# A four-layer graph network kernel: keys and queries of the top-p attention made while the features are made, second step on features already multiplied by U

## The chip, the cores and the metric

The kernel runs on one core of a Trainium2 chip. The metric is the device time of one launch in microseconds (us); lower is better. All data is float32, apart from a few throw-away outputs in bfloat16.

The engines that matter here: TensorE (PE in the profile, its weight loads PEld), VectorE (DVE), ScalarE (ACT), GpSimd (POOL) and SyncE (SP), which here only issues DMAs. Each engine runs its own list of instructions strictly in order and waits on semaphores for the results of others. PE's clock is granted by a throttle: 1.00 is full speed, 0.50 half.

## The reference, cut to what matters

A graph of n = 3327 nodes has features x (n x 256) and a sparse weight matrix adj (n x n, about 1% of its entries not zero, stored in full). Four layers follow each other, each with a residual and a layer normalization: x = layernorm(x + layer(x)). Layer 0 aggregates neighbours, layer 1 is a graph convolution with a Mamba scan, layer 2 a graph attention, layer 3 is this:

```
R = S + eye(N);  R = R / R.sum(-1, keepdims=True)        # S is adj
Z = 0; Xf = X; Xa = X
for n in range(2):
    q = Xa @ W1.T @ W2.T;  k = Xa @ W3.T                 # N x 64 each
    A = softmax(q @ k.T), in each row only the largest entries up to
        a mass of 0.9 are kept, then each row is divided by its sum
    Xf = R @ Xf
    Xa = A @ Xa
    Z = Z + Xf @ U1[n].T + Xa @ U2[n].T
return layernorm(X + Z)
```

The change concerns layers 2 and 3 alone. Layer 3 has two kinds of large products per step: the diffusion R @ Xf, and the attention A @ Xa, whose matrix A must first be made: logits, softmax, and for every row the threshold that keeps 0.9 of the mass (the search).

## The kernel before, in words

Nodes are cut into nt = 26 row tiles of 128. X, the features, stays in SBUF as 26 tiles of 128 x 256; adj is streamed, transposed by the host, tile by tile, in every stage that needs it: a row tile needs 26 blocks of 128 x 128. The code is written in order of tiles; a scheduler then gives each engine a fixed order of its instructions, and it does move work of neighbouring tiles past each other. Tiles of memory come from pools with a fixed number of buffers, which sets how far a load or a copy may run ahead.

**Layer 2** (`layer2`, L516 on): for each row tile, two halves of 13 blocks are loaded, DVE makes the weights from each in place (two operations on 128 x 1664), and 26 matmuls add up `acc` (L549). Then, per tile, a chain over DVE, ACT and POOL makes the new X: L552 to L561 on DVE and ACT, mean and variance at L77 and L78, the power on POOL (L565, L566), and last `X` on POOL (L567). Adding `acc` takes 26 matmuls, each of them two records in the trace.

**Layer 3** is two calls of `one_pass` (L927): pass 1 with X as attention source, `search_short` and `first`; pass 2 with Xa, `search_long` and `second`. A pass goes:

- `keys` (L607): for all 26 tiles, one after another, two transposes (L94), a copy on ACT (L96), two matmuls with W3 (L613), a copy into kT (L615). Nothing else of the pass can start before it. The weights W1, U1, U2, W2, W3 are loaded ahead of pass 1 (L61, L581, L582), after layer 2 in SP's queue.
- per tile `query` (L618): transposes, W1 (L622), W2 (L626), with an ACT copy after each; `logits` (L631): eight matmuls (L642), 416 columns wide, contraction of 64, each copied by ACT into `e` (L643).
- the search. `search_short` (L685): the eight largest of each segment of 128 (L650), six rounds of ranking (L659, L661), one exponential over the row (L668) that also gives the sum, then the threshold v and the masked row. `search_long` (L697) is in three stages, which run for three different tiles in each step of the loop (lead 2, 1, 0): stage 1 makes two exponentials (L712, L713); stage 2 estimates a threshold with a Sign count and a masked sum (L723, L725), then a better one with Relu and Sign (L747, L748); stage 3, from L750 on, takes the count, masks (L769), ranks, settles ties (L788) and masks again (L789).
- the attention product, `attend` (L111): the row tile `e` is transposed in 26 pieces (L118), copied out in groups of four (L120) and multiplied with X or Xa (L122). L805 scales the sum.
- the diffusion, `diffuse` (L864) with `aggregate` (L99): loads of 9 blocks, 26 matmuls (L107), and L869 adds the tile itself.
- in pass 2, `finish` (L877): four sources are transposed (L94, L96) and multiplied by U1 and U2 of both steps, eight matmuls (L884); then two layer normalizations (L886 to L897), and the store.
- at the pass's end `unresolved` (L901) finds whether a certificate of the search fails for any tile. The flag is read by all engines (L946), and a branch would run such tiles again in an exact and slow way.

Of the kernel before, what the change touches and what calls it, by code (L numbers as in the profile page):

```python
# [15 lines left out]
PSUM = bass.MemoryType.PSUM  # L16

# [14 lines left out]
LN15 = math.log(1.5)  # L32
# [3 lines left out]
HUGE = 1e38  # L36
KC = 416
# [3 lines left out]
def gnn_kernel(ctx: ExitStack, tc: tile.TileContext, n: int, a: dict, out: bass.AP):  # L41
# [369 lines left out]
    def layer2_any():  # L411

        with tc.tile_pool(name="l2", bufs=1) as pool, tc.tile_pool(name="l2w", bufs=2) as work, \
                tc.tile_pool(name="l2p", bufs=3, space=PSUM) as psum:
            wg = load(pool, "gat_w")
            asr, ads = (load_row(pool, x) for x in ("attn_src", "attn_dst"))
            H = pool.tile([P, nt, D], F32, name="H")
            col = pool.tile([P, nt, 2], F32, name="col")
            src = pool.tile([P, npad], F32, name="src")
            mv_all = pool.tile([P, nt, 2], F32, name="mv_all")  # L420
            rs_all = pool.tile([P, nt], F32, name="rs_all")
            for it in range(nt):
                xt = transposed(work, psum, X[:, it, :], "xt")
                po = psum.tile([P, D], F32, name="acc")
                for k in range(2):
                    nc.tensor.matmul(po, xt[:, k, :], wg[:, k, :], start=(k == 0), stop=(k == 1))
                nc.scalar.copy(H[:, it, :], po)
                for k, v in enumerate((asr, ads)):
                    scr = work.tile([P, D], F32, name="scr")
                    nc.vector.scalar_tensor_tensor(scr, H[:, it, :], 1.0, v, op0=ALU.mult, op1=ALU.mult,  # L430
                                                   accum_out=col[:, it, k:k + 1])

            for j0 in range(0, nt, 4):
                m = min(4, nt - j0)
                pt = psum.tile([P, 4, P], F32, name="ps")
                for j in range(m):
                    nc.tensor.transpose(pt[:, j, :], col[:, j0 + j, 0:1].to_broadcast([P, P]), ident)
                nc.scalar.copy(src[:, j0 * P:(j0 + m) * P], pt[:, :m, :].rearrange("p a b -> p (a b)"))
            for it in range(nt):
                ad = work.tile([P, n], F32, name="ad")  # L440
                nc.sync.dma_start(ad, a["adj"][it * P:(it + 1) * P, :])
                s = work.tile([P, npad], F32, name="s", bufs=3)
                if npad > n:
                    nc.vector.memset(s[:, n:], 0.0)
                sn = s[:, :n]
                nc.scalar.activation(sn, src[:, :n], AF.Identity, bias=col[:, it, 1:2])
                nc.vector.scalar_tensor_tensor(sn, sn, 0.2, sn, op0=ALU.mult, op1=ALU.max)
                nc.vector.scalar_tensor_tensor(sn, ad, 0.0, sn, op0=ALU.is_gt, op1=ALU.mult)
                neg = small.tile([P, 1], F32, name="neg")
                nc.vector.reduce_max(neg, sn, axis=AX.X)  # L450
                nc.vector.tensor_scalar_mul(neg, neg, -1.0)
                nc.scalar.activation(sn, sn, AF.Exp, bias=neg)
                den = small.tile([P, 1], F32, name="den")
                nc.vector.scalar_tensor_tensor(sn, ad, 0.0, sn, op0=ALU.is_gt, op1=ALU.mult, accum_out=den)
                nc.vector.tensor_scalar_add(den, den, 1e-8)
                nc.vector.reciprocal(den, den)
                acc = attend(work, psum, s, H)
                o = work.tile([P, D], F32, name="o")
                nc.vector.tensor_scalar_mul(o, acc, den)

                ex = work.tile([P, D], F32, name="ex")
                nc.vector.tensor_scalar_min(ex, o, 0.0)
                nc.scalar.activation(ex, ex, AF.Exp)
                nc.vector.scalar_tensor_tensor(o, o, 0.0, X[:, it, :], op0=ALU.max, op1=ALU.add)
                nc.vector.scalar_tensor_tensor(X[:, it, :], ex, -1.0, o, op0=ALU.add, op1=ALU.add)
                stats(mv_all[:, it, :], X[:, it, :])
            rstd_of(rs_all, mv_all[:, :, 1])
            for it in range(nt):
                standardize(X[:, it, :], X[:, it, :], mv_all[:, it, 0:1], rs_all[:, it:it + 1])
# [6 lines left out]
    with tc.tile_pool(name="l2c", bufs=1) as pool:  # L476
        col = pool.tile([P, nt, 2], F32, name="col")
        V = pool.tile([P, nt, D + 1], F32, name="V")
        fit = pool.tile([1, 1], I32, name="fit")
        with tc.tile_pool(name="l2a", bufs=1) as wpool, tc.tile_pool(name="l2w", bufs=2) as work, \  # L480
                tc.tile_pool(name="l2p", bufs=3, space=PSUM) as psum:
            wg = wpool.tile([P, 2, D + 2], F32, name="wg")
            nc.sync.dma_start(wg[:, :, :D], a["gat_w"])
            for k, v in enumerate(("attn_src", "attn_dst")):
                r = load_row(wpool, v)
                for i in range(2):
                    scr = work.tile([P, D], F32, name="scr")
                    nc.vector.scalar_tensor_tensor(scr, wg[:, i, :D], 1.0, r, op0=ALU.mult, op1=ALU.mult,
                                                   accum_out=wg[:, i, D + k:D + k + 1])
            for it in range(nt):  # L490
                xt = transposed(work, psum, X[:, it, :], "xt")
                po = psum.tile([P, D + 2], F32, name="acc")
                for k in range(2):
                    nc.tensor.matmul(po, xt[:, k, :], wg[:, k, :], start=(k == 0), stop=(k == 1))
                nc.vector.tensor_copy(col[:, it, :], po[:, D:])
                g = V[:, it, D:]
                nc.scalar.activation(g, col[:, it, 0:1], AF.Exp, scale=0.2)
                nc.scalar.mul(V[:, it, :D], po[:, :D], g)

            big = wpool.tile([P, nt, 2], F32, name="big")  # L500
            nc.scalar.activation(big, col, AF.Abs)
            m = wpool.tile([P, 2], F32, name="m")
            nc.vector.reduce_max(m, big.rearrange("p t k -> p k t"), axis=AX.X)
            pm = psum.tile([2, P], F32, name="ps")
            nc.tensor.transpose(pm, m, ident)
            m2 = wpool.tile([2, 1], F32, name="m2")
            nc.vector.reduce_max(m2, pm, axis=AX.X)
            one = wpool.tile([2, 1], F32, name="one")
            nc.vector.memset(one, 1.0)
            ps = psum.tile([1, 1], F32, name="ps")  # L510
            nc.tensor.matmul(ps, m2, one, start=True, stop=True)
            f = wpool.tile([1, 1], F32, name="f")
            nc.vector.tensor_scalar(f, ps, BIG, None, op0=ALU.is_le)
            nc.vector.tensor_copy(fit, f)

        def layer2():  # L516
            with tc.tile_pool(name="l2", bufs=1) as pool, tc.tile_pool(name="l2w", bufs=2) as work, \
                    tc.tile_pool(name="l2at", bufs=5) as atp, \
                    tc.tile_pool(name="l2p", bufs=3, space=PSUM) as psum:
                q = pool.tile([P, nt], F32, name="q")  # L520
                nc.scalar.activation(q, col[:, :, 0], AF.Exp, scale=0.8)
                eps = pool.tile([P, nt], F32, name="eps")
                nc.scalar.activation(eps, col[:, :, 1], AF.Exp, scale=-1.0)
                nc.vector.tensor_scalar_mul(eps, eps, 1e-8)
                mhalf = pool.tile([P, 1], F32, name="mhalf")
                nc.vector.memset(mhalf, -0.5)

                r = pool.tile([P, npad], F32, name="r")
                for j0 in range(0, nt, 4):
                    m = min(4, nt - j0)  # L530
                    pt = psum.tile([P, 4, P], F32, name="ps")
                    for j in range(m):
                        nc.tensor.transpose(pt[:, j, :], col[:, j0 + j, 1:2].to_broadcast([P, P]), ident)
                    nc.scalar.activation(r[:, j0 * P:(j0 + m) * P], pt[:, :m, :].rearrange("p a b -> p (a b)"),
                                         AF.Exp, scale=-0.8)
                for it in range(nt):
# [493 lines left out]
```

## Time and profile before

| | |
|---|---|
| median of 3 runs | 4331.85 us (4331.15 to 4336.95) |
| the profiled execution | 4330.06 us |
| its span, first to last instruction | 4327.9 us |
| mean granted PE clock | 0.927 |
| PE busy | 3880.5 us, 90% |
| DVE busy | 2795.9 us, 65% |
| ACT busy | 1731.7 us, 40% |
| POOL busy | 276.6 us, 6% |
| moved by DMA | 239.33 MB, mean 55 GB/s |

The stages, in us from the span's start: layer 0 to 361; layer 1 and the projection of layer 2 to about 1830; layer 2's aggregation 1855.8 to 2149.9; keys of pass 1 to 2223.2; pass 1 to 3095.2; flag and keys of pass 2 to 3163.2; pass 2 to 4327.9.

How to read the profile: busy times are sums over the whole span, and an engine can be busy in one stage and wait in the next, so the stages are read apart. A row of a group gives line, engine, operation, output and inputs, how often, then busy time and mean, then the idle time that this engine had just before such instructions and what ended it. In a line of the timeline the first number is the start, the second the time from that start to the end of the group, and the bracket is the idle time before it and its releaser.

### The profile page before, as it was taken

The numbers are of one execution on the slowest core, as the hardware profiler recorded it, in microseconds if no ns is written. First come the engines' busy times: TensorE is split into PE (matmuls) and PEld (weight loads), VectorE is DVE, ScalarE is ACT, GpSimd is POOL, SyncE is SP. The second block draws the span as 40 slices with busy tenths as digits, with TensorE's granted clock in tenths as the row PEclk, the third lists the DMA queues.
The fourth block names the chain that finished last, engine by engine and source line by source line (L and its number), as shares of the span: only waits on it lengthen the run. The fifth ranks groups of instructions, "written<-read, shape, count | busy, mean of one in ns | idle before, by whom it ended". The sixth has DMA issues, their size and how long they took to land. (4 is left out here: it accounts for less than half of the span.)

```text
span 4327.9 us, 42860 instructions
## 1 busy us (share of the span) xinstructions
PE 3880.5 (90%) x15597; PEld 2791.7 (65%) x15597; DVE 2795.9 (65%) x6159; ACT 1731.7 (40%) x2826; POOL 276.6 (6%) x344
## 2 busy tenths in 40 slices
PE   8998999999999977799889999999868889888988
PEld 7886644444444433588767777777646767676767
DVE  1111588888888899688624444444158877787784
ACT  0001444444444544510033333333265656565652
POOL 0000000000000010133300000000000000000000
PEclk9998898989898988899969999999869999999999
DMA  5443211111111000044301111111101111111111
GB/s 180 136 141 98 68 37 32 37 32 32 32 32 32 21 0 0 21 159 152 131 16 48 48 53 59 48 48 49 32 0 51 41 46 40 46 40 46 41 45 37
DMA packets 67053, 239.33 MB, mean 55 GB/s; under 512 B 8434, under 2 KB 22770, under 8 KB 66690
## 3 DMA queue, kind: packets, MB, share of 16 engines
q1 hardware_dynamic: 66818, 236.37, 17.1%
q8 instruction: 127, 2.08, 0.2%
q14 instruction: 108, 0.88, 0.1%
HBM read 232.93 MB, written 3.41 MB: 55 GB/s over the span
## 5 line engine op out<-in xcount | busy, mean ns | idle before, releaser
L393 PE MATMUL y<-h,ident 128*128 128x512 f32 (+1 forms) x896 | 466.4, 671 | 91.3 <-DVE h L342 91.3
L339 DVE TENSOR_TENSOR_SCAN h<-dA,carry,db 128x512 f32<-128x512 f32 (+1 forms) x448 | 511.6, 1193 | 4.8 <-DVE db L336 0.5
L328 ACT ACTIVATE dA<-dt,A_log 128x512 f32<-128x512 f32 (+1 forms) x448 | 281.4, 684 | 350.8 <-DVE h L339 333.1
L393 PEld LDWEIGHTS y<-h,ident 128*128 128x128 f32 x896 | 192.2, 225 | 354.2 <-issue 206.4
L204 PE MATMUL cb<-X,at 128*128 128x256 f32 x1352 | 334.6, 403 | 26.9 <-ACT h L221 14.7
L204 PEld LDWEIGHTS cb<-X,at 128*128 128x128 f32 x1352 | 270.1, 203 | 113.7 <-issue 52.2
L122 PE MATMUL acc<-Xa,wt 128*128 128x256 f32 x1352 | 322.3, 391 | 19.3 <-ACT wt L120 18.9
L122 PE MATMUL acc<-X,wt 128*128 128x256 f32 x1352 | 310.1, 383 | 10.7 <-ACT wt L120 8.7
L107 PE MATMUL acc<-xa,at 128*128 128x257 f32 x1352 | 308.3, 381 | 0.0
L107 PE MATMUL acc<-Xf,at 128*128 128x256 f32 x1352 | 307.6, 379 | 0.0
L107 PE MATMUL acc<-X,at 128*128 128x256 f32 x1352 | 304.3, 379 | 0.0
L122 PEld LDWEIGHTS acc<-Xa,wt 128*128 128x128 f32 x1352 | 260.4, 196 | 67.3 <-ACT wt L120 31.9
L642 PE MATMUL ps<-kT,q 64*128 64x416 f32 x832 | 254.8, 595 | 54.2 <-ACT e L643 31.6
L549 PE MATMUL acc<-V,at 128*128 128x257 f32 x1352 | 294.2, 379 | 1.4 <-DVE at L546 1.4
L336 DVE TENSOR_TENSOR db<-du,row 128x2048 f32<-128x2048 f32 (+1 forms) x112 | 238.9, 2133 | 82.8 <-ACT row L324 82.6
L122 PEld LDWEIGHTS acc<-X,wt 128*128 128x128 f32 x1352 | 252.4, 190 | 59.5 <-ACT wt L120 27.3
L549 PEld LDWEIGHTS acc<-V,at 128*128 128x128 f32 x1352 | 255.8, 189 | 39.8 <-DVE at L546 1.8
L107 PEld LDWEIGHTS acc<-xa,at 128*128 128x128 f32 x1352 | 255.6, 191 | 37.5 <-issue 0.7
L96 ACT COPY xt<-ps 128x256 f32<-128x256 f32 x234 | 82.0, 373 | 491.3 <-PE ps L94 436.8
L107 PEld LDWEIGHTS acc<-X,at 128*128 128x128 f32 x1352 | 253.0, 190 | 32.3
L107 PEld LDWEIGHTS acc<-Xf,at 128*128 128x128 f32 x1352 | 251.4, 190 | 31.3
L321 PE MATMUL ps<-dbc,ident 48*128 48x512 f32 (+1 forms) x448 | 234.3, 637 | 20.3 <-ACT row L324 19.8
(273 smaller groups left out, 5698.6 us busy)
## 6 DMA issues: line engine op xcount, KB each, us to landing
at<-in_adjT SPq DMA_DIRECT2D x156, 576.0 KB, 3.7
at<-in_adjT SPq DMA_DIRECT2D x104, 832.0 KB, 4.4
at<-in_adjT SPq DMA_DIRECT2D x78, 512.0 KB, 3.5
xa<-in_x SPq DMA_DIRECT2D x1, 3328.0 KB, 12.7
xt<-in_xT SPq DMA_DIRECT2D x26, 128.0 KB, 3.9
out<-h SPq DMA_DIRECT2D x25, 128.0 KB, 1.7
w_in<-in_w_in SPq DMA_DIRECT2D x1, 1024.0 KB, 5.4
U<-in_U SPq DMA_DIRECT2D x2, 512.0 KB, 6.1
```

Of the source, the lines that this page charges most:

```text
L96: nc.scalar.copy(t, pt)
L107: nc.tensor.matmul(acc, at[:, j, :], rhs[:, j0 + j, :], start=(j0 + j == 0), stop=(j0 + j == nt - 1))
L122: nc.tensor.matmul(acc, wt[:, j, :], rhs[:, j0 + j, :], start=(j0 + j == 0), stop=(j0 + j == nt - 1))
L204: nc.tensor.matmul(acc, at[:, j % JC, :], X0[:, j, :], start=(j == 0), stop=(j == nt - 1))
L321: nc.tensor.matmul(ps[:, :w], ident[:R, r:r + 1].to_broadcast([R, P]), dbc[:, :w], start=True, stop=True)
L328: nc.scalar.activation(dA[:, g, :], dt[:, g, :], AF.Exp, scale=A[:, g, s:s + 1])
L336: nc.vector.tensor_mul(db, du, bc[0])
L339: nc.vector.tensor_tensor_scan(h[:, g, :], dA[:, g, :], db[:, g, :], initial=carry[:, s, g:g + 1], op0=ALU.mult, op1=ALU.add)
L393: nc.tensor.matmul(ys[g][:, :w], ident, h[:, g, :], start=(s == 0), stop=(s == DS - 1))
L549: nc.tensor.matmul(acc, at[:, j, :], V[:, j0 + j, :], start=(j0 + j == 0), stop=(j0 + j == nt - 1))
L642: nc.tensor.matmul(pl[:, :w], q[a:a + DA, :], kT[a:a + DA, c0:c0 + w], start=True, stop=True)
```

## The change

Nothing is approximated: the same sums are made in another order. The new code

- makes `wq`, the product of W1 and W2, once before layer 2, and loads W1, W2 and W3 there (ahead of layer 2's weights in SP's queue);
- in layer 2, after the first 13 matmuls of tile `it`, makes key and query of tile `it - 1` for pass 1 (`project`). The key goes to `kT[0]`, the query to DRAM (`qd`), from which each pass loads one tile at a time;
- in pass 1, makes in `first`, for every tile and directly from Xf and Xa of this tile: s = X + Xf U1[0] + Xa U2[0], which goes to DRAM (`sd`); Y = Xf U1[1]; G = Xa U2[1]; and key and query of the tile for pass 2;
- in pass 2, diffuses Y and applies the attention to G, so that their sum with s is already X + Z: `second` has no matmuls and no transposes, and only the layer normalizations;
- runs the diffusion up to DL = 4 tiles ahead and in groups of J3 = 7 blocks, one group after each pair of logits matmuls (`both`); `first` and `second` of a tile end one step of the loop later;
- has no barrier between the passes; the flags of both are tested once, at the end (L1051 of the new file);
- in `search_long`, puts some scalar steps that don't need the second count ahead of the end of stage 2; the exponential of pass 1 has no offset any more.

The exact path for flagged tiles and the other path of layer 2 (`layer2_any`) are changed to suit. The diff, cut to its core:

```diff
+        wk = pool.tile([P, 2, 2 * DA], F32, name="wk")
+        wq = pool.tile([P, 2, 2 * DA], F32, name="wq")
...
+        def key_and_query(work, ps, p, it, xt):
+
+            for k in range(2):
+                nc.tensor.matmul(ps[:, 0, :], wk[:, k, :], xt[:, k, :], start=(k == 0), stop=(k == 1))
+            h, j = divmod(it * P, half)
+            nc.scalar.copy(kT[p][h * DA:(h + 1) * DA, j:j + P], ps[h * DA:(h + 1) * DA, 0, :])
+            nc.sync.dma_start(qd[p][it], query(work, ps[:, 1, :], xt))
...
+                    def project(it):
+                        xt = transposed(work, psum, X[:, it, :], "xt")
+                        key_and_query(work, psum.tile([P, 2, P], F32, name="ps"), 0, it, xt)
...
+                            if j0 == 0 and it:
+                                project(it - 1)
...
+                    project(nt - 1)
...
-        def keys(work, psum, xs):
...
-        def query(work, psum, xs, it):
...
-        def finish(work, psum, it, xf2, xa2):
...
+        def aggregated(atp, psum, it, rhs):
+
+            acc = psum.tile([P, D], F32, name="acc")
+            for j0 in range(0, nt, J3):
...
+                yield None
+            yield acc
...
+        def diffused(work, atp, psum, p, it, out):
+
+            rd = rdeg[:, it:it + 1]
+            t = work.tile([P, D], F32, name="t")
+            nc.gpsimd.tensor_scalar(t, (Y if p else X)[:, it, :], rd, None, op0=ALU.mult)
+            if p:
+                s = work.tile([P, D], F32, name="s")
+                nc.sync.dma_start(s, sd[it])
+                nc.gpsimd.tensor_tensor(t, t, s, op=ALU.add)
+            for acc in aggregated(atp, psum, it, Y if p else X):
+                if acc is None:
+                    yield
+            d = work.tile([P, D], F32, name="xf", bufs=DL + 2)
+            nc.vector.scalar_tensor_tensor(d, acc, rd, t, op0=ALU.mult, op1=ALU.add)
+            out.append(d)
...
+        def first(work, psum, it, acc, f, xf):
+
+            xa = work.tile([P, D], F32, name="xa")
+            nc.scalar.mul(xa, acc, f)
+            yield
+            pt = psum.tile([P, 4, P], F32, name="pj")
+            for i, v in enumerate((xf, xa)):
+                for k in range(2):
+                    nc.tensor.transpose(pt[:, 2 * i + k, :], v[:, k * P:(k + 1) * P], ident)
+            xt = work.tile([P, 4, P], F32, name="xt", bufs=1)
+            nc.scalar.copy(xt, pt)
...
+            for k in range(4):
+                nc.tensor.matmul(ps[:, 0, :], xt[:, k, :], (u1 if k < 2 else u2)[:, 0, k % 2, :],
+                                 start=(k == 0), stop=(k == 3))
+            for k in range(2):
+                nc.tensor.matmul(ps[:, 1, :], xt[:, k, :], u1[:, 1, k, :], start=(k == 0), stop=(k == 1))
+            for k in range(2):
+                nc.tensor.matmul(pg[:, 0, :], xt[:, 2 + k, :], u2[:, 1, k, :], start=(k == 0), stop=(k == 1))
+            s = work.tile([P, D], F32, name="s")
+            nc.vector.tensor_add(s, ps[:, 0, :], X[:, it, :])
+            nc.sync.dma_start(sd[it], s)
+            nc.scalar.copy(Y[:, it, :], ps[:, 1, :])
+            nc.scalar.copy(G[:, it, :], pg[:, 0, :])
+            key_and_query(work, pg[:, 1, :].rearrange("p (a b) -> p a b", a=2), 1, it, xt[:, 2:, :])
+            yield
+
+        def second(work, psum, it, acc, f, xf):
+
+            h = work.tile([P, D], F32, name="h")
+            nc.vector.scalar_tensor_tensor(h, acc, f, xf, op0=ALU.mult, op1=ALU.add)
+            yield
...
+            for p, search, step, lead in ((0, search_short, first, (1,)), (1, search_long, second, (2, 1, 0))):
+                es, searches, xfs, todo = {}, {}, [], None
+                for i in range(-lead[0], nt):
+                    t = i + lead[0]
+                    parts = []
+                    if t < nt:
+                        q = work.tile([2 * DA, P], F32, name="q")
+                        nc.sync.dma_start(q, qd[p][t])
+                        es[t] = work.tile([P, npad], F32, name="e", bufs=3)
...
+                        parts.append(scores(work, psum, p, q, es[t]))
+                    more = range(len(xfs), min(nt, i + DL + 1))
+                    for j in more[:1]:
+                        parts.append(diffused(work, atp, psum, p, j, xfs))
+                    both(*parts)
+                    for part in lead:
+                        if 0 <= i + part < nt:
+                            next(searches[i + part])
+                    for j in more[1:]:
+                        both(diffused(work, atp, psum, p, j, xfs))
+                    if todo is not None:
+                        next(todo)
+                    if i >= 0:
...
+                        todo = step(work, psum, i, attended(work, psum, es[i], G if p else X), f, xfs[i])
+                        next(todo)
+                next(todo)
...
-        one_pass(X, search_short, first, (1,))
-        one_pass(Xa, search_long, second, (2, 1, 0))
```

## The prediction, made before the change had run

> **What bounds the kernel now.** The span is 4327.9 us; the profiled execution took 4330.06 us, so 2.2 us lie around the span, and it stands 1.8 us under the median of 4331.85. I first cut the span into stages (windows: length; then busy us of PE, PEld, DVE, ACT, POOL; then PE's clock, DMA share and GB/s).
>
> ```profile
> 1830.00:2150.00 320.00, 314.96 (x1453) 272.97 (x1452) 246.10 (x299) 35.33 (x99) 96.56 (x75) 0.99 0.41 139
> 2150.00:2223.00 73.00, 45.17 (x164) 33.88 (x164) 3.44 (x42) 19.22 (x58) 3.93 (x8) 0.53 0.14 45
> 2223.00:3098.00 875.00, 829.45 (x3998) 662.54 (x3998) 394.99 (x1414) 306.06 (x570) 24.39 (x47) 1.00 0.16 49
> 3098.00:3165.00 67.00, 47.26 (x169) 35.05 (x170) 0.00 (x0) 17.33 (x56) 1.77 (x5) 0.52 0.00 1
> 3165.00:4328.00 1163.00, 1004.60 (x4618) 789.68 (x4617) 885.56 (x3000) 659.36 (x881) 86.40 (x177) 0.94 0.13 40
> ```
>
> Layer 2's aggregation (row 1) and pass 1 (row 3) are PE at full clock with little slack: 11.4 and 33.4 us per tile of 26. Rows 2 and 4 make keys, serially, at half clock. Pass 2 (row 5) is busy on PE for 86%, DVE 76%, ACT 57%: none is full, engines wait for each other. Next I read the starts of the two serial stages and one DVE wait of pass 2 on the timeline, and the list of waits for that pass (us in total, times, longest).
>
> ```profile
> 2164.04 1.20 PE L613 MATMUL ps<-xt,w 128*128 128x128 f32 x4 [11.82 <-DMA w<-in_W]
> 3101.16 0.66 PE L94 MATMUL ps<-ident,Xa 128*128 128x128 f32 x2 [5.74 <-PEq L946]
> 3724.38 0.15 DVE L750 TENSOR_SCALAR k<-sg 128x1 f32<-128x1 f32 x1 [6.24 <-ACT ajunk L748]
> ```
> ```profile
> DVE k L750 <- ACT ajunk L748: 152.8, 26, 7.6
> PE ps L94 <- DVE xf L869: 38.8, 24, 2.0
> ```
>
> The weights for the keys are loaded only when layer 2 is over; the flag test costs 5.7 us; DVE, the busiest engine of a pass-2 cycle, still stands 152.8 us for the Sign count of L748. Last, the rows of section 5 that price what is moved (busy us, mean ns of one).
>
> ```profile
> L642 PE MATMUL ps<-kT,q 64*128 64x416 f32 x832 | 254.8, 595 | 54.2 <-ACT e L643 31.6
> L884 PE MATMUL acc<-U,xt 128*128 128x256 f32 x416 | 113.7, 421 | 8.0 <-ACT xt L96 6.0
> L668 ACT ACTIVATE e<-e,neg 128x3328 f32<-128x3328 f32 x26 | 79.8, 3071 | 39.3 <-DVE neg L667 36.1 <-DVE f L799 3.2
> L725 DVE SCALAR_TENSOR_TENSOR djunk<-e,c 128x3328 bf16<-128x3328 f32 x26 | 95.5, 3675 | 0.1
> L788 DVE MATCH_REPLACE8 e<-rep,e 128x1664 f32<-128x1664 f32 x52 | 97.1, 1875 | 0.0
> L567 POOL TENSOR_SCALAR X<-o,mv,rs 128x256 f32<-128x256 f32 x26 | 69.8, 2685 | 2.7
> ```
>
> **What the Trainium skill says.** "TensorE: Matmul & The Clock Gate", section "What's actually happening": the array falls to half clock after an idle window of about 3.4 us and comes back after a window as long of sustained work. The trace agrees on the return (after a gap of 3.96 us at 706 to 710 the clock was 0.50 for 5 us, then 0.71, and some 3.8 us of work were lost) but is harsher on the fall: gaps of 2.3 to 3.1 us were followed by slow matmuls too, and after one of 1.68 us the eight U matmuls took 3.34 us, not 1.99. The pair below, the same eight matmuls behind a long and a short gap, shows a loss of 1.7.
>
> ```profile
> 618.86 5.40 PE L393 MATMUL y<-h,ident 128*128 128x512 f32 x8 [3.12 <-DVE h L342]
> 631.35 3.70 PE L393 MATMUL y<-h,ident 128*128 128x512 f32 x8 [0.22 <-DVE h L342]
> 3731.38 3.34 PE L884 MATMUL acc<-U,xt 128*128 128x256 f32 x8
> ```
>
> "DMA: Bandwidth & Descriptors", section "Anatomy of one DMA — SWDGE (gpsimd) path": a transfer has a fixed cost near 2 us, most of it the receipt for its last write. That bears on the query's trip to DRAM and back; the page's DMA list has 1.7 us for a 128 KB store, and no row here shows a store that is read back.
>
> **The change, part by part.**
>
> *Setup.* W1·W2 is merged once and three weight loads go ahead of layer 2's on SP's queue: 0 to 5 us, I take +3.
>
> *Layer 2.* Each tile but the last gets a projection of the tile before, amid its matmuls: 2 transposes (0.22 us), 2 + 2 matmuls 128 wide (0.48 each) and 0.17 of a wait for a copy: 1.35 x 25 = +34, as PE has no slack here. It also stands too early. PE's order has it at matmul 13 of 26, 13 x 0.438 = 5.7 us after the last aggregation's end, and X of that tile takes longer: with DVE idle, at the stage's end, aggregation ends at 2149.93 and POOL's L567 at 2155.62, 5.7; beside DVE's masks L567 takes 2.69 in place of 1.23, so 7.1 to 7.4. PE stalls about 1.5 x 25 = +37. Gaps of this size lie at the edge of the clock's fall; I take +11 (none: 0; each with 1.7: +42). Behind the waiting transposes stand 13 matmuls, and no engine waits for them but this chain. Sum +82 (50 to 115). The q store on SP's queue stands behind both loads of its tile, and five buffers cover the next: 0.
>
> *The gap after layer 2.* 73.3 us go (26 keys x 2.17, the 11.8 for W, the first query). What stays: last X 5.7, its projection at half clock 3, q store and load about 2 each, the branch's end about 2: 15. So -58 (-50 to -63).
>
> *Pass 1.* PE's work per tile: diffusion 11.4 and attention 11.4 (52 records of 0.219 each), 26 transposes 3.1, logits about 3.5; new here are 4 transposes 0.44, 8 U matmuls of 256 columns at about 0.43, 3.5, and the key and query of pass 2 at about 1.1. The sum is 34.4, against 33.4 before, which held the query's three round trips through ACT. The new wait is ACT's order: the exponential of tile i+1 (L750 after; L668 before) now stands ahead of the copy `xt` of `first` (L866), for which PE's U matmuls wait. Counted from the tile's last logits matmul: copies end at 0.8, the last segment maxima, first ranking and `neg` end near 2.5 (0.2 x 3, 0.38, 0.45, 0.14), the exponential takes 3.07 + 0.18 and the copy 0.58, to 6.3 or, with releases, 6.5. PE in that time has five matmuls (2.2), 4 transposes (0.44) and 8 more (0.9): 3.5. A stall of 3.0 per tile (2 to 4). All of `attended` and the next tile's logits queue behind it on PE. Such a gap costs clock: 2.2 a tile, between the 1.7 and 3.8 above. So 39.6 x 26 = 1030, + 12 for a first lead and four last tiles without diffusion; before, 872. Hence +170 (+75 to +235).
>
> *Between the passes.* Flag readback and keys, 68 us, go; Y's first five diffusions (52 us) stand there instead. Counted with pass 2.
>
> *Pass 2.* `finish` leaves: 8 transposes and 8 U matmuls, about 9 us of PE with its gaps. PE keeps 29 per tile, ACT 23, DVE 35: three full-width products (L725, L769, L789: 3.68 each), 2 x 1.88 of L788, the rest as in a cycle of before, where 44.2 less 9.1 of idle left 35.1. Does the idle for L748 go? It came from ACT running behind PE's finish and logits; with the 9 us of finish out of that ring I take 35.4 for the ring of copies, Sign and Relu, and with some clock loss before each tile's transposes 36.3 (35.1 to 39). From the last `first`: tile 0's attention ends at 94 (five diffusions 52, three sets of logits 9, attention 14.5, and DVE's stages of tile 0, which also wait for the fifth diffusion), tile 1's weights at 104, tile 25's at 104 + 24 x 36.3 - 8 = 967, + 31 of tail as before (4297 to 4328) = 998. Before: 1164.7 + 68 = 1232.7. So -235 (-170 to -264).
>
> *Sum:* 3 + 82 - 58 + 170 - 235 = -38 on 4330.06, 4292; against the median, 4294.
>
> **Rivals.** All turn on PE's gaps.
> *The clock holds.* The stalls are as drawn, but none pulls the clock down: -57 in pass 1, -11, -29 in pass 2: 4197. For it: 1.58 us was once harmless, and the pass-1 row stands at 1.00. Against: 2.3 to 3.1 was not.
> *The slower side: each gap costs a whole cold window.* Pass 1 loses 3.8, not 2.2 (+42), and each stall of layer 2 1.7, not 0.45 (+31): 4367. The two gaps lie in the same place of every tile, amid long PE work. It decides from 38 us on, 0.75 per tile over 51 tiles.
> *The Sign wait stays.* DVE keeps its 6.2 us per tile in pass 2: 41.3 x 24, +120: 4414. Against it: nothing of PE's old finish stands before the copies.
> *The certificate fires.* Should rounding raise a flag, whole tiles run again, some hundreds of us. Before, with such sums, none did.
>
> **Chances.** My forecast 0.48 (its own range 4250 to 4345), the clock holds 0.22, whole window 0.20, Sign wait 0.08, flag 0.02. A measurement here tells 0.2%, 8.7 us, from no change. Faster: 0.33 of the forecast's cases and 0.22: 0.55; same 0.08; slower 0.07 + 0.30 = 0.37. The range from 4190 to 4400 leaves out about half of the first rival below and about half of the Sign wait with the flag above.
>
> **What would show it.** Layer 2: PE waiting for POOL's X near 1.5 us a tile, stage near 376. Pass 1: PE's L870 waiting for ACT's L866 near 3 a tile with the clock under 1.00, pass 1 near 1040. Pass 2: DVE near 95% in the steady part, cycle near 36, and L750's successor waiting little for Sign. Wrong it would be if pass 1 ran under 37 or over 42 a tile, or the cycle of pass 2 were over 39.

## The result, and the profile after

The changed kernel is slower: 4361.86 us, the median of 4 runs (4353.43 to 4364.85), against 4331.5 before; the ratio is 1.0064, 95% interval 1.0047 to 1.0082. The forecast was 4294, so its sign was wrong. The profiled execution took 4353.43 us (span 4351.6) against 4330.06 before, 23.4 more. The other three runs took some 8 us longer; what the profiles show of a scatter of that size is told with the last repetition below.

The windows of the changed kernel, cut at its own stages (columns as before: length, busy us of PE, PEld, DVE, ACT, POOL, then PE's clock, DMA share, GB/s):

```profile
1859.80:2239.80 380.00, 337.72 (x1602) 283.28 (x1602) 249.88 (x277) 41.83 (x125) 85.03 (x75) 0.98 0.34 115
2239.80:2255.20 15.40, 3.19 (x13) 2.23 (x12) 2.26 (x7) 2.96 (x6) 4.01 (x8) 0.66 0.08 17
2255.20:3310.60 1055.40, 980.16 (x4545) 760.80 (x4546) 401.22 (x1389) 335.54 (x623) 27.28 (x53) 0.96 0.17 51
3310.60:4351.60 1041.00, 867.86 (x3781) 648.11 (x3779) 852.82 (x2950) 600.41 (x677) 178.96 (x202) 0.89 0.17 50
```

The rows are layer 2's aggregation, the gap behind it, pass 1 (to the last key and query of pass 2), pass 2. PE had no idle time in row 1 before and some 43 us in row 3, at a clock of 1.00 in both; now it has 42 us in row 1 and 75 in row 3, and a clock below 1.00 in both. Set against the forecast:

| stage (us) | before | after | difference | forecast |
|---|---|---|---|---|
| up to layer 2's aggregation, and it | 294 from 1855.8 | 380.0 from 1859.8 | +90 | +85 |
| gap after layer 2 | 73.3 | 15.4 | -58 | -58 |
| pass 1 | 872 | 1055.4 | +183 | +170 |
| flag, keys, pass 2 | 1232.7 | 1041.0 | -192 | -235 |
| sum | | | +23 | -38 |

So the gap closed as foretold, and pass 2 gained, but 43 us less; layer 2 and pass 1 lost what was foretold and 18 us more. The timelines show each loss at work. In layer 2 the projection's transposes (L96) wait for X of the tile before:

```profile
2046.65 0.44 PE L96 MATMUL ps<-ident,X 128*128 128x128 f32 x2 [1.69 <-POOL X L621]
2061.22 0.44 PE L96 MATMUL ps<-ident,X 128*128 128x128 f32 x2 [1.75 <-POOL X L621]
```

The starts lie 14.6 us apart: 11.4 of aggregation, 1.7 of waiting, the rest the projection. One tile of pass 1 on PE, cut to what follows:

```profile
2602.40 1.04 PE L700 MATMUL tp<-ident,e 128*128 128x128 f32 x8
2606.73 3.62 PE L870 MATMUL pj<-U,xt 128*128 128x256 f32 x8 [3.29 <-ACT xt L866]
2610.19 1.03 PE L873 MATMUL pj<-U,xt 128*128 128x256 f32 x4
...
2617.41 0.96 PE L660 MATMUL sc<-kT,q 64*128 64x416 f32 x2
...
2622.82 0.96 PE L660 MATMUL sc<-kT,q 64*128 64x416 f32 x2
...
2631.47 0.97 PE L660 MATMUL sc<-kT,q 64*128 64x416 f32 x4
2632.37 3.29 PE L672 MATMUL acc<-X,at 128*128 128x256 f32 x14
```

PE waits 3.29 us for the copy `xt`, and the next group starts 3.46 us after L870's start, where 1.83 is usual (below): a slow clock, 1.6 us. The last lines show logits (two records to a matmul): a pair that lies together takes 0.90 from start to start, and so does a single matmul. In pass 2, the DVE and ACT lines of one cycle of 37.5 us:

```profile
3885.37 0.16 DVE L902 SCALAR_TENSOR_TENSOR nb<-mv,rs 128x1 f32<-128x1 f32 x1 [0.76 <-POOL rs L442]
3889.25 0.15 DVE L741 TENSOR_SCALAR lim<-tot 128x1 f32<-128x1 f32 x1 [2.25 <-ACT e L771]
```
```profile
3885.57 0.60 ACT L903 ACTIVATE h<-h,nb,rs 128x256 f32<-128x256 f32 x1 [1.25 <-DVE nb L902]
3886.07 3.05 ACT L771 ACTIVATE e<-e,neg 128x3328 f32<-128x3328 f32 x1
```

The last normalization of a finished tile (Identity, L903) stands on ACT ahead of the exponential of another tile (L771). DVE waits for POOL's power, ACT for DVE's `nb`, the exponential for that, and DVE for the exponential's sum. PE is caught as well: the copies `wt`, which its attention product needs, stand behind the same exponential on ACT.

```profile
3889.74 5.54 PE L704 MATMUL acc<-G,wt 128*128 128x256 f32 x16 [3.02 <-ACT wt L702]
3895.12 1.04 PE L700 MATMUL tp<-ident,e 128*128 128x128 f32 x8
```

After the wait of 3.02 these sixteen records take 5.38 from start to start; the next sixteen of the same tile (3896.43 to 3899.96) take 3.53. So each cycle has some 1.9 us of slow clock on PE too.

### The profile page after: what moved, and what is told of

The parts are those of the page before. It is cut to its first block, busy times and chain, and to the rows that moved or that the text cites. A ratio compares the mean times of both kernels' runs of the same rounds, so it can differ in the third digit from the quotient of the medians.

```text
span 4351.6 us, 42124 instructions
## 1 busy us (share of the span) xinstructions
PE 3849.4 (88%) x15239; PEld 2709.8 (62%) x15239; DVE 2778.8 (64%) x6060; ACT 1692.5 (39%) x2648; POOL 358.3 (8%) x370
## 5 line engine op out<-in xcount | busy, mean ns | idle before, releaser
L712 DVE MAX8 cand<-e 128x8 f32<-128x128 f32 x676 | 143.8, 279 | 586.0 <-ACT e L661 585.7
L704 PE MATMUL acc<-G,wt 128*128 128x256 f32 x1352 | 367.4, 429 | 75.6 <-ACT wt L702 75.0
L704 PEld LDWEIGHTS acc<-G,wt 128*128 128x128 f32 x1352 | 283.2, 216 | 154.9 <-ACT wt L702 111.7
L661 ACT COPY e<-sc 128x416 f32<-128x416 f32 (+1 forms) x416 | 192.8, 508 | 435.2 <-PE sc L660 435.2
L702 ACT COPY wt<-tp 128x512 f32<-128x512 f32 (+1 forms) x364 | 188.6, 552 | 445.9 <-PE tp L700 445.4
L704 PE MATMUL acc<-X,wt 128*128 128x256 f32 x1352 | 322.9, 384 | 2.9 <-ACT wt L702 2.8
L672 PE MATMUL acc<-Y,at 128*128 128x256 f32 x1352 | 324.4, 386 | 0.0
L672 PE MATMUL acc<-X,at 128*128 128x256 f32 x1352 | 320.2, 386 | 0.5 <-DMA at<-in_adjT 0.5
L602 PE MATMUL acc<-V,at 128*128 128x257 f32 x1352 | 311.8, 384 | 2.7 <-DVE at L599 2.7
L672 PEld LDWEIGHTS acc<-Y,at 128*128 128x128 f32 x1352 | 246.2, 190 | 72.1 <-issue 43.0
L109 PEld LDWEIGHTS acc<-xa,at 128*128 128x128 f32 x1352 | 254.9, 190 | 37.1 <-issue 0.7
```

What stands on the lines that cost most here:

```text
L109: nc.tensor.matmul(acc, at[:, j, :], rhs[:, j0 + j, :], start=(j0 + j == 0), stop=(j0 + j == nt - 1))
L602: nc.tensor.matmul(acc, at[:, j, :], V[:, j0 + j, :], start=(j0 + j == 0), stop=(j0 + j == nt - 1))
L661: nc.scalar.copy(e[:, c:c + w], pl[:, :w])
L672: nc.tensor.matmul(acc, at[:, j, :], rhs[:, j0 + j, :], start=(j0 + j == 0), stop=(j0 + j == nt - 1))
L702: nc.scalar.copy(wt[:, :m, :], pt[:, :m, :])
L704: nc.tensor.matmul(acc, wt[:, j, :], rhs[:, j0 + j, :], start=(j0 + j == 0), stop=(j0 + j == nt - 1))
```

## Experiments

Every experiment starts from the changed kernel; ratios are to the kernel before on the same chip. Where a comparison with the changed kernel is drawn, its medians are 4361.86 and, in a second set, 4362.66.

### The projection later in layer 2

```diff
-                            if j0 == 0 and it:
+                            if j0 and it:
                                 project(it - 1)
```

> The projection of tile it-1 is put after the second half of tile it's aggregation instead of the first. Theory (the stall is the chain to X, which needs 7.4 us and gets 5.7): PE's wait for POOL's X, 1.7 us on nearly every tile of layer 2, goes; the cycle of layer 2 falls from 14.6 to about 12.9, the stage from 380 us to about 338, the whole from 4353 to about 4312. Rival (the chain is slow because PE's own transposes and copies delay it, so that it moves along): the cycle stays above 14. A second rival, that the clock fell after these gaps, would give more than 1.8 us a tile.

Measured: 4311.89 us, ratio 0.9957 (0.9941 to 0.9974), 50 under the changed kernel; the stage took 343.8 us. The list of waits has, for the changed kernel,

```profile
PE ps L96 <- POOL X L621: 47.7, 22, 5.7
```

and for this one

```profile
PE ps L96 <- POOL X L621: 12.7, 4, 3.8
```

The theory holds: the chain to X is what PE waited for, and 13 more matmuls cover it in all but three of the first six tiles and the last projection. A steady tile now takes 12.6 us, 1.3 more than before (294.1 / 26 = 11.3): that is the projection's own work. The rest of the 50 us by which the stage is longer than before (343.8 - 294) is waiting in those first tiles (9 us) and slow clock (0.97 over the stage). The place where the projection stood costs 36 us more in the profiles and 50 in the medians; the profile of this run is the slowest of its four. The second rival isn't excluded by the medians, 50 / 25 = 2.0 us a tile: the next experiment shows clock loss in layer 2.

### The copy for the U matmuls taken off the queue of the exponential

```diff
-            nc.scalar.copy(xt, pt)
+            nc.vector.tensor_copy(xt, pt)
```

> The copy xt in first is made by VectorE instead of ScalarE, so that it no longer stands behind the exponential of the next tile; all else as in the changed kernel. Theory (the exponential ahead of xt costs the wait of 3.3 us and then 1.7 us of slow U matmuls): the cycle of pass 1 falls from 40.95 to about 36.0, the eight matmuls of L870 from 3.6 to 2.0, the whole by about 22 x 5 = 110 to 4243. Rival (the wait moves to the wt copies, which also stand behind the exponential): the cycle stays at 38 to 40 with PE waiting for wt, a gain of 20 to 60.

Measured: 4282.35 us, ratio 0.9890 (0.9874 to 0.9907), 80 under the changed kernel, where 110 were expected. Pass 1 took 972.4 us in place of 1055.4, its cycle 36.90 in place of 40.95:

```profile
2634.27 1.04 PE L700 MATMUL tp<-ident,e 128*128 128x128 f32 x8
2636.13 1.99 PE L870 MATMUL pj<-U,xt 128*128 128x256 f32 x8 [0.82 <-DVE xt L866]
2637.96 1.03 PE L873 MATMUL pj<-U,xt 128*128 128x256 f32 x4
```

The wait is 0.82 and the eight records of L870 (four matmuls; the prediction and the expectations count records here) take 1.83 from start to start. So the exponential ahead of `xt` cost 2.5 + 1.6 = 4.1 us a tile, less than the 5 foretold since DVE takes 0.8 to get to the copy; the rival's wait for `wt` isn't there.

The same profile shows layer 2, which this edit doesn't touch, in part in another rhythm: 399.0 us.

```profile
2057.41 0.69 PE L96 MATMUL ps<-ident,X 128*128 128x128 f32 x2 [4.50 <-POOL X L621]
2057.89 1.92 PE L602 MATMUL acc<-V,at 128*128 128x257 f32 x4
...
2071.72 0.44 PE L96 MATMUL ps<-ident,X 128*128 128x128 f32 x2
2072.00 1.03 PE L602 MATMUL acc<-V,at 128*128 128x257 f32 x4
```

One tile waits 4.5 us and loses clock (1.92 for four records in place of 1.03), the next waits not at all. Over the pair that is 31 to 32 us, where two waits of 1.7 make 29.2. Six tiles of the 26 wait so (3.9 to 4.7 us); in the first profile of the changed kernel it is one.

### The diffusion of pass 1 behind the logits, not amid them

```diff
-                    both(*parts)
+                    if p:
+                        both(*parts)
+                    else:
+                        for part in parts:
+                            both(part)
```

> In pass 1 alone the logits of a tile come first and its diffusion after them, not one group after each pair. Theory (the interleaving itself brings the exponential onto PE's path, as only 2.2 us of diffusion are left behind the last logits): with 11.8 us of diffusion behind them the wait for xt goes, -5.0; the logits become bound by ScalarE's copies, +0.5 to +1: a cycle near 36.5 to 37, the whole near 4353 - 22 x 4.2 = 4260. Rival (interleaving pays more than it costs, since copies at 0.51 each would hold PE up by more): a cycle of 39 or more.

Measured: 4293.69 us, ratio 0.9921 (0.9905 to 0.9938), 68 under the changed kernel, where the expected 4260 was 93 under 4353; pass 1 took 985.4 us, its cycle 37.41. PE's logits and L870 in one tile:

```profile
2655.82 0.97 PE L660 MATMUL sc<-kT,q 64*128 64x416 f32 x4
2657.37 1.37 PE L660 MATMUL sc<-kT,q 64*128 64x416 f32 x4 [0.59 <-ACT e L661]
2658.93 1.37 PE L660 MATMUL sc<-kT,q 64*128 64x416 f32 x4 [0.19 <-ACT e L661]
...
2672.40 1.99 PE L870 MATMUL pj<-U,xt 128*128 128x256 f32 x8
```

The wait for `xt` is gone, though ACT's order is the same: the diffusion now lies between the last logits and L870, and covers the exponential. The price is that the logits wait for ACT's copies: the pairs follow each other every 1.56 us in place of 0.90, and the cycle is 37.41 where PE's own work takes 36.0 (worked out below). So this one part of the change, undone alone, gives back 70 us of the 183 that pass 1 lost: the interleaving hides ACT's copies, which cost little, and uncovers ACT's exponential, which costs much.

### The row halves of the logits apart

```diff
-            for c0 in range(0, half, KC):
-                for h in (0, DA):
+            for h in (0, DA):
+                for c0 in range(0, half, KC):
```

> The eight logits matmuls of a tile come in the order of columns: all of the first row half of the array, then all of the second, where before they alternate. Same work, same copies. Theory (two neighbours that use different halves of the rows run at the same time: a pair takes 0.90 us, a single one 0.89): the three pairs of pass 1 that still lie together come apart, +0.9 x 3 = 2.7 us a tile, pass 1 by about 60 us slower; pass 2, bound by VectorE, by 0 to 20; the whole near 4415 to 4435. Rival (they don't overlap, the single ones take so long for another reason): no change, 4353.

Measured: 4378.43 us, ratio 1.0111 (1.0094 to 1.0128), 17 over the changed kernel; pass 1 took 1061.2 us, 5.8 more and not 60, with a median cycle of 40.59, which is shorter than before. Neither side's number came.

```profile
2614.18 1.66 PE L660 MATMUL sc<-kT,q 64*128 64x416 f32 x4
2615.77 3.29 PE L673 MATMUL acc<-X,at 128*128 128x256 f32 x14
...
2631.65 1.99 PE L871 MATMUL pj<-U,xt 128*128 128x256 f32 x8 [2.53 <-ACT xt L867]
2633.48 1.03 PE L874 MATMUL pj<-U,xt 128*128 128x256 f32 x4
```

The theory's premise is right: a pair now takes 1.59 from start to start in place of 0.90, so neighbours in different halves do overlap, and three pairs add 2.1 us of work. But it filled idle time: the wait for `xt` fell by 0.76, and after the wait of 2.53 the clock fell in only 4 of 21 tiles (3.25 to 3.36 for the eight records), which gave 1.6 back in the others. From the first tile's L871 to the 21st's the stage took 818.7 us, and 819.0 with L870 in the changed kernel: the added work cost nothing there. The 5.8 us arose ahead of the first tile's U matmuls; why stays open. What a piece of work costs here depends on the gap that follows it. Pass 2 took 3.7 us more; the other 7 or 8 of the 17 aren't in layer 3; layer 2 took 394.5 us in this profile, and more on its scatter follows below.

### The last normalization on GpSimd

```diff
-            nb = small.tile([P, 1], F32, name="nb")
-            nc.vector.scalar_tensor_tensor(nb, mv[:, 0:1], -1.0, rs, op0=ALU.mult, op1=ALU.mult)
-            nc.scalar.activation(h, h, AF.Identity, scale=rs, bias=nb)
+            nc.gpsimd.tensor_scalar(h, h, mv[:, 0:1], rs, op0=ALU.subtract, op1=ALU.mult)
```

> In second, the last normalization runs on GpSimd as one (h - mean) x rs, in place of nb on VectorE and Identity on ScalarE. Theory: in the changed kernel ScalarE stands 1.25 us in each cycle of pass 2 for nb, which itself waits for GpSimd's power, with the exponential of the next tile queued behind it; VectorE then waits 2.25 us for the exponential's sum and 0.76 for the power. Taken away, the cycle of 37.5 falls to about 35, pass 2 by 24 x 2.3 = 55 us, the whole from about 4360 to about 4305. Rival (the ring of ScalarE has no slack, and the wait for the Sign count in L814, 1.4 us now, grows by what the other loses): the cycle stays above 36.8, gain under 20.

Measured: 4320.83 us, median of 16 runs, ratio 0.9977 (0.9969 to 0.9985), 42 under the changed kernel; pass 2 took 999.6 us in place of 1041.0. Its cycles now alternate between 34.4 and 37.3 us, where those of the changed kernel are near 37.5 in the steady part; from tile 1's weights to tile 25's the mean is 35.3 in place of 37.1. The waits of DVE, counted between 3450 and 4280 us of each profile, were in the changed kernel

```profile
DVE lim L741 <- ACT e L771: 42.5, 19, 2.3
DVE k L814 <- ACT junk L801: 31.4, 22, 2.4
DVE nb L902 <- POOL rs L442: 16.4, 21, 1.3
```

and are here

```profile
DVE lim L741 <- ACT e L771: 30.3, 10, 3.0
DVE k L783 <- ACT junk L780: 15.9, 19, 1.1
DVE k L814 <- ACT junk L801: 11.9, 12, 2.6
```

The theory holds for the place and most of the size (41 of 55). Part of it moved, as the new row for L783 shows, but the Sign wait of L814 fell too, against the rival. PE's waits for `wt` fell with them, from 67.9 to 8.7 us in the same stretch. The edit takes away the wait of the exponential together with the wait and slow clock of PE behind it, so their shares in the 41 us aren't separated.

### Pass 2 one tile ahead, not four

```diff
-                    more = range(len(xfs), min(nt, i + DL + 1))
+                    more = range(len(xfs), min(nt, i + (1 if p else DL) + 1))
```

> In pass 2 alone the diffusion runs one tile ahead and not four. Theory: at the start of pass 2 VectorE, which works in a fixed order, stands 3 + 13 us for sums of the first five diffusions while the search of tile 0 is queued behind; with two diffusions instead of five, tile 0's weights are ready about 16 to 20 us earlier (66 to 70 us after the last key and query of pass 1 in place of 86), the second tile's likewise; the cycle of 37.5 doesn't change and the whole falls by 15 to 25. Rival (the start is set by the chain of the three stages over VectorE and ScalarE): under 8.

Measured: 4345.64 us, median of 14 runs, ratio 1.0037 (1.0027 to 1.0047), 17 under the changed kernel. Tile 0's weights are ready 66.1 us after the last key and query in place of 86.0, tile 1's 98.0 in place of 118.1; the cycle is 37.54 as before; pass 2 is 16.7 shorter. The theory holds. In the changed kernel DVE's first stages of pass 2 had stood behind sums of the diffusion:

```profile
3346.24 0.48 DVE L690 SCALAR_TENSOR_TENSOR xf<-acc,rdeg,t 128x256 f32<-128x256 f32 x1 [3.17 <-PE acc L672]
3361.84 0.48 DVE L690 SCALAR_TENSOR_TENSOR xf<-acc,rdeg,t 128x256 f32<-128x256 f32 x1 [13.40 <-PE acc L672]
```

### All four, and the changed kernel again

The edits of the first, second, fifth and sixth experiment together.

> Projection late in layer 2, xt on VectorE, last normalization on GpSimd, pass 2 one tile ahead, all together. Theory (four stalls in four places, in stages that follow each other): the gains add up, 45 + 80 + 55 + 20 = 200 from about 4360, to about 4160. Rival (in pass 2 the two edits act on the same wait): 30 to 50 less than that, 4190 to 4210.

Measured: 4172.13 us, ratio 0.9626 (0.9610 to 0.9642), 190 under the changed kernel measured beside it and 158 under the kernel before. Layer 2 took 344.2, pass 1 971.5, pass 2 979.6 us. The gains of the four alone, 50 + 80 + 42 + 17 = 189, add up.

> The changed kernel as it is, once more, beside the others. Its runs so far lay between 4353 and 4365. Theory: layer 2 has two rhythms, one in which every tile waits 1.7 us for X at full clock (380 us for the stage, as in its first profile) and one in which a tile waits 4.5 us, loses clock, and the next waits not at all (395 to 399 us, as in the profiles of the kernels with another pass 1); so a stage of 380 goes with about 4353, one of 395 with about 4365. Rival: the difference lies elsewhere, and the stages of layer 3 differ.

Measured: 4362.66 us (4356.36 to 4368.98), ratio 1.0078 (1.0062 to 1.0095). Pass 1 took 1055.2 and pass 2 1041.0 us in its profile, as in the first, and layer 2 387.2. Over the seven profiles with the projection in its first place layer 2 took 380.0, 387.2, 394.5, 395.4, 396.5, 399.0 and 386.2 us, while pass 1 and pass 2 agreed within 2 us in all but one of the profiles in which their code was the same. One is apart: pass 1 of the first experiment, the same code, took 1060 us. So most of the scatter lies in layer 2, as the theory has it, and some ahead of it, as the stage began anywhere from 1855.2 to 1863.3 us. It isn't two clean rhythms: 386 and 387 lie between. The length goes with the granted clock of the stage: 0.98 in the profile of 380.0 us, 0.97 in those of 386.2 and 387.2, 0.95 in those of 394.5 and 395.4, 0.94 in those of 396.5 and 399.0. PE ran at half clock for 13.7 us in the shortest and for 47.8 in the longest, and half of the difference is 17 of the 19 us. What starts the longer waits was not found, and that the runs without a profile scatter for the same reason is not shown.

### The logits pairs kept whole

```diff
-                    both(*parts)
+                    both(*(parts if p else parts[::-1]))
```

This is put on top of the four edits.

> The kernel with all four edits, and in pass 1 each group of the diffusion now stands ahead of the pair of logits matmuls and not behind it, so that the first pair is no longer pulled apart among attention's matmuls. Theory (a pair that is split costs 0.89 us more, as its two halves then don't run together): the cycle of pass 1 falls from 36.90 to about 36.0, or to 35.2 if the wait of 0.8 for xt goes too; pass 1 by 20 to 40 us, the whole from 4172 to about 4135 to 4150. Rival (with the last pair at the end of the tile the exponential comes 2.2 us later and holds up the wt copies or the Y and G copies instead): no gain, or up to 30 us slower.

Measured: 4152.15 us, ratio 0.9580 (0.9564 to 0.9596); pass 1 took 954.8 us in place of 971.5, its cycle 36.10 in place of 36.90. That is a little less than the 20 to 40 us, and the 4135 to 4150, that were expected; layer 2, which the edit doesn't touch, was 6 us shorter in this profile.

```profile
2601.80 0.97 PE L660 MATMUL sc<-kT,q 64*128 64x416 f32 x4
2602.70 2.43 PE L672 MATMUL acc<-X,at 128*128 128x256 f32 x10
2605.06 0.97 PE L660 MATMUL sc<-kT,q 64*128 64x416 f32 x4
...
2607.78 1.13 PE L704 MATMUL acc<-X,wt 128*128 128x256 f32 x4 [0.29 <-ACT wt L702]
2608.89 1.99 PE L870 MATMUL pj<-U,xt 128*128 128x256 f32 x8
```

All pairs lie together, and PE waits 0.5 in all (another 0.23 stands further on). The gain of 0.8 a tile is about the 0.89 that a split pair costs; the wait for `xt` went too, but waits for `wt` and G took most of its place, so the two can't be told apart to the tenth. This is the fastest version of the study, 181 us under the kernel before.

## Why the prediction was wrong, point by point

All five steps had the right direction; the forecast of -38 was the difference of +255 and -293, and misses of 61 us in sum turned its sign.

- *Setup and layer 2*, +85: measured +90 in the profiled run. Of these, 4 are a later start (3 were forecast), 42 PE's waits for X, 1.7 a tile (37, 1.5 a tile), about 7 slow clock (11), and the remaining 37 the projection's work (34). The later projection confirmed the cause of the waits. That layer 2 has longer waits in other profiles was not foreseen: they add up to 19 us.
- *The gap*, -58: measured -58, with some luck in the terms. X came after 5.7 as forecast, but the projection took 4.0 and not 3, the store and the load of the query held PE for 5.6 and not 4, and the 2 for the end of a branch didn't come.
- *Pass 1*, +170: measured +183. The stall was 3.3 where 3.0 was said, the slow clock 1.6 where 2.2 was said. The step that failed is "The sum is 34.4", PE's own work: 40.95 - 3.29 - 1.63 = 36.0 a tile, not 34.4. The logits take five times 0.90, as the scheduler pulls one pair apart, and not 3.5; the diffusion takes 11.8, and not 11.4. That is 1.4 to 1.6 a tile, some 40 us; 21 of them were given back, as the last four tiles, without a diffusion, made the end shorter (1055 is 9 less than 26 cycles) where 12 us had been added for start and end, and 7 by stall and clock.
- *Pass 2*, -235: measured -192. The step that failed is "I take 35.4 for the ring of copies, Sign and Relu, and with some clock loss before each tile's transposes 36.3". From tile 1's weights to tile 25's the mean cycle was 37.1, not 36.0 (27 us); in the steady part it was 37.5. The forecast's ring has no term for the layer normalization of `second`, whose steps over POOL, DVE and ACT stand in front of an exponential, and it has 0.9 for the clock. What the traces show is that DVE waits for that chain and for the exponential, and that PE waits 3.0 for the copies behind it and then loses 1.9 to the clock. The fifth experiment took the normalization off ACT and got 41 us. Another 14 were the start: tile 1's weights came at 118, not 104, after the diffusions that the forecast itself had named; the sixth experiment shows that running them so far ahead costs 17 to 20. In one cycle (3852.10 to 3889.65) DVE was busy for 32.8 us of 37.55, 87% and not 95, and PE for 33.1, where 29 had been kept for it. The prediction had also called DVE the busiest engine of a cycle before, against its own row for pass 2: PE 86%, DVE 76%.

The slower rival, 4367, lies near the measured time, but by luck: the clock loss in pass 1 was smaller than in the forecast, not larger, and in the profiled run layer 2 kept most of its clock (0.98). Slow matmuls in layer 2, of which it spoke, do appear in the profiles with the longer waits, in some tiles and not in all. "The clock holds" is refuted by L870 in pass 1. The Sign wait didn't stay at 6.2 us a cycle: L814 waited 1.4. The certificate didn't fire: after pass 2 nothing follows in the profile.

What the clock page of the Trainium skill says of the fall ("TensorE: Matmul & The Clock Gate", section "What's actually happening": about 3.4 us of idle time) is near what pass 1 of the changed kernel shows, where the clock fell after all 21 waits of 3.3 to 3.5. But the length of a wait alone doesn't decide: of the 21 waits near 2.5 in the fourth experiment four were followed by a fall, and of 21 waits of 1.7 in pass 2 of the kernel before five; the 1.68 that the prediction cites is one of these, and not the usual case.

The traces hold a pattern that the forecast didn't use. In each of the eleven, all changes of PE's clock lie on a regular grid of 3.41 us. Here are three windows of the changed kernel on that grid, the wait for `xt` and the two stretches behind it (columns as above):

```profile
2603.20:2606.60 3.40, 0.23 (x3) 0.00 (x0) 3.16 (x13) 3.40 (x4) 0.92 (x1) 1.00 0.39 129
2606.65:2610.00 3.35, 3.27 (x8) 2.65 (x9) 2.84 (x7) 1.32 (x4) 0.00 (x0) 0.50 0.00 0
2610.10:2613.40 3.30, 3.30 (x18) 2.96 (x18) 2.54 (x5) 0.37 (x1) 0.00 (x0) 1.00 0.03 11
```

In the fourth experiment the clock fell in the four tiles where the wait began 1.17 to 1.39 us into a stretch of the grid, so that at least 2.0 of its 3.41 us were idle, and kept up in the 17 where it began later (1.42 to 2.44). That the idle time within one stretch decides fits these waits; no experiment moved a wait against the grid to test it. The cycles fit the grid as well: 40.96 us in pass 1 of the changed kernel are 12 stretches, 37.55 in pass 2 are 11, and the 34.4 and 37.3 of the fifth experiment together are 21. How much of a cycle in pass 2 is the clock's and how much the normalization's stays open.

## What to carry to other kernels

Before work is put amid other work to hide one engine's short copies, look at what the old order was hiding: here a block of diffusion behind the logits covered an exponential of 3 us on another engine, and with only a part of it left the exponential fell on the bound engine's path. Any instruction that waits on a chain over several engines (a normalization, a power, a scale) should not be queued ahead of a long instruction that others wait for; the engine with free time can take it whole. And where a forecast is a small difference of large gains and losses, its sign is open, however good each part is.

## What was not expected of the hardware

- Two logits matmuls with a contraction of 64, in different row halves of the array, take 0.90 us from start to start for the pair, and 1.59 for two in the same half; one alone takes 0.89.
- After a wait of 3.29 the eight records of L870 took 3.46 us in place of 1.83, and after one of 0.82 they took 1.83; after waits of 2.53 four tiles of 21 were slow. In the first experiment, after the same wait of 3.29, L870 took 2.55 to 3.02 and the next eight records 2.69 to 2.22 in place of 1.73, so the slow stretch had moved on while its cost stayed near 1.7.
- Added work of 2.1 us a tile on the engine that bounds a stage made the median cycle 0.36 shorter, and 20 tiles took 818.7 us in place of 819.0, as the gap behind it seldom cost clock.
